# Second-product weights of a Mamba-style block in six buffers of two chunks instead of two buffers of six

## The chip, the cores and the metric

The kernel runs as one program on one core of a Trainium2 chip. The metric is the time of one execution on the device in microseconds (us); a change is judged by the median of repeated runs.

## What is computed

The input x is 8 images of 384 channels by 1024 positions, in fp32. One layer of two parts is applied:

```python
x = x + conv(ln_c(x), ...)          # the Mamba-style part, all 8 images
t = to_tokens(x)
t = t + ffn(ln_t(t), W1, b1, W2, b2)
x = from_tokens(t, x)
```

The first part normalises over channels twice, multiplies by in_proj (384 to 2 x 768), runs a causal convolution with 3 taps and SiLU over one half, derives step sizes and the rows B and C, and scans 16 states per inner channel along the 1024 positions:

```python
hst = dA_t * hst + dBu_t            # per position, 16 states per inner channel
y_t = einsum("bdn,bn->bd", hst, C_t)
y = (y + xc * D) * silu(z)
t = y @ out_proj_w.T                                        # 768 -> 384
t = gelu(t @ mlp_w1.T + mlp_b1) @ mlp_w2.T + mlp_b2         # 384 -> 1536 -> 384
```

The second part (FFN) binarises two weight matrices by the sign against a group mean, multiplies 384 to 1536, scales and clips by the largest absolute value, takes GELU, multiplies 1536 to 384 and scales and clips again. Only the first 5 of the 8 images get non-zero work in it.

## The kernel before, in words

**Tiling.** A matmul takes a 128x128 block of weights and 128x512 moving values in fp32. Channels lie on partitions in chunks of 128 (KC = 3 chunks of 384, KD = 6 of 768, KH = 12 of 1536, HK = 6 is half of KH), positions in two halves of T = 512. PER = 2 is the number of chunks in one activation tile: `split` (L459) makes a list of tiles of two chunks.

**Stages.** For each image b, `s1` (L670) normalises, multiplies by in_proj and makes xc, z, dt and dt*xc, and stores them to DRAM. `s2` (L835) with `scan` (L848) and `scan_pair` (L957) loads them back, spread over states, and scans on VectorE, with products on GpSimd (POOL), exponentials on ScalarE (ACT) and the sum over states on TensorE (tile `py`). `s3` (L1024) does out_proj (tile `p_out`), the first MLP product (`p_h`), GELU and the second MLP product (`p_o`). `ffn` (L1228) does the same for the FFN (`p_y`, which is written from `tn` in the first product and from `gf` in the second). `norm` (L590) is the normalisation used by `s1` and `ffn`.

**The order.** Nothing is issued in the order of the code. Each stage calls `Plan.add` (L201) with an engine, a cost in us, the tiles read and written and a function that emits the instructions. `Plan.run` (L248) is a list scheduler that runs while the program is built: it keeps a simulated time for PE, ACT, DVE, POOL and SP, takes the operation that can start first, picks among those able by `choose` (L274) and `rank` (L291: scans first, then the earliest batch), and emits it. The order in which it emits is each engine's program order on the chip; on the chip, semaphores hold every instruction until its inputs are there. A DMA in the plan costs its issue on SP, then `size / rate` on one shared transfer resource, then `land` (L370 to L373). Where the plan sees PE idle for over IDLE = 0.7 us, it fills the hole with small matmuls into a free PSUM tile named `spare` (L347 to L356, emitted at L451); their results are not used.

**Buffers.** `Ring` (L130) is a set of equal buffers. A tile takes one when its first operation starts and gives it back when the last operation that reads it has ended. Weights come through `weights` (L530), which makes one tile and one DMA load (`load`, L508, the load itself is L511, on SP). The rings of the two second products and of out_proj are made at L419; each buffer of six chunks holds 6 x 128 fp32 values per partition (384 KB in all), and the two rings hold two such buffers each:

```python
"w6": ring("w6", 2), "w6_n": ring("w6_n", 2), "res": ring("res", 4),
```

`w6` serves out_proj and the second MLP product, `w6_n` the FFN's second product and one third of out_proj in the last batch. In the profile their tiles are called `w` and `w_n`. The other products use tiles of three chunks, `w_f` and `w_b`.

**Where the tiles are used.** `mlp_out` (L1098) makes one PSUM tile from twelve chunks: it loads two tiles of six chunks, and adds three PE operations of two matmuls each per tile (`matmuls`, L536). So a weight tile is held until its third operation ends. out_proj adds one PE operation of six matmuls per output chunk (L1058 on); in the last batch five of the six matmuls are issued early, and the sixth when the scan's last tile is there (L1032 to L1054, the list `late`). The loads wait for a buffer, so SP, which issues in program order, stands at such a load until PE has read the old tile for the last time.

Of the kernel before, what the change touches and what calls it, by code (L numbers as in the profile page):

```python
# [35 lines left out]
KC = C // P  # L36
DI = 768
KD = DI // P
# [4 lines left out]
HK = KH // 2  # L43
PER = 2
T = 512
# [26 lines left out]
MM = 0.859  # L72
# [23 lines left out]
def c_dve(n):  # L96
    return 0.17 + n * 0.00102
# [71 lines left out]
class Fixed:  # L169


    ring = None
# [218 lines left out]
class Layer:  # L391
    def __init__(self, ctx, tc, a, out):
        self.tc, self.nc, self.a, self.out = tc, tc.nc, a, out
        self.plan = Plan()

        def pool(name, **kw):
            return ctx.enter_context(tc.tile_pool(name=name, bufs=1, **kw))

        self.const = pool("const")
        sbuf, psum, dram = pool("sbuf"), pool("psum", space=PSUM), pool("dram", space=DRAM)  # L400

        def ring(tag, bufs, where=sbuf):
            def make(shape, name):
                return where.tile(shape, F32, tag=tag, name=name, bufs=bufs)

            return Ring(make, bufs)

        self.rings = {

            "front": ring("front", 6), "t_f": ring("t_f", 2), "w_f": ring("w_f", 4),  # L410
            "dbc": ring("dbc", 1), "halo": ring("halo", 2),

            "dt_r": ring("dt_r", 2), "dtx_r": ring("dtx_r", 2), "u": ring("u", 3),
            "xr": ring("xr", 1), "zr": ring("zr", 1), "state": ring("state", 1),
            **{f"bc{i}": ring(f"bc{i}", 1) for i in range(2 * NQUAD)},
            "da": ring("da", 2, psum), "y": ring("y", 1, psum),

            "hid": ring("hid", 9), "t_b": ring("t_b", 1), "w_b": ring("w_b", 3),
            "w6": ring("w6", 2), "w6_n": ring("w6_n", 2), "res": ring("res", 4),  # L419

            "t_n": ring("t_n", 2), "small": ring("small", 4),

            "mm": ring("mm", 3, psum), "sq": ring("sq", 2),
            "rstd": ring("rstd", 2), "root": ring("root", 2),
        }

        def handed(name, shape):
            return Fixed(dram.tile(shape, F32, name=name))

        self.dram = {}  # L430
        for b in range(B):
            self.dram["dt", b] = handed(f"dt_d{b}", [DI, L])
            self.dram["dtx", b] = handed(f"dtx_d{b}", [KC, P, 2 * L])

            for name in ("xc", "z", "yg"):
                self.dram[name, b] = handed(f"{name}_d{b}", [KD, 2, P, T])
            self.dram["rows", b] = handed(f"rows_d{b}", [2 * NS, L])
            if b < NQ:
                self.dram["mid", b] = handed(f"mid_d{b}", [C, L])
                self.dram["y1", b] = handed(f"y1_d{b}", [P, KH, L])  # L440
        self.bin = {
            "W1": handed("bin_w1", [KH, P, KC, P]), "W2": handed("bin_w2", [KC, P, KH, P]),
        }
        self.constants()

        first = psum.tile([P, T], F32, tag="y", name="first", bufs=1)
        self.nc.tensor.matmul(
            first, self.ones, self.one.to_broadcast([P, T]), start=True, stop=True
        )
        self.plan.spare = self.piece("mm", [P, T], "spare")  # L450
        self.plan.fill = lambda: self.nc.tensor.matmul(  # L451
            self.plan.spare.real[:, : 2 * P], self.ones,
            self.one.to_broadcast([P, 2 * P]), start=True, stop=True,
        )
# [135 lines left out]
    def norm(self, t, eps, scale):  # L590

        nc, add = self.nc, self.plan.add
        def columns(src, name):
            p = self.piece("mm", [P, TG], name)

            def emit():
                for k in range(KC):
                    for g in range(G):
                        nc.tensor.matmul(
                            p.real[g * DQ : (g + 1) * DQ, :], self.ones[:, :DQ],  # L600
                            src.real[:, k, g * TG : (g + 1) * TG],
                            start=(k == 0), stop=(k == KC - 1),
                        )

            add("PE", 0.79, emit, r=[src], w=[p], tiled=True)
            return p

        def spread(src, name, turned=False):
            p = self.piece("mm", [P, T], name)

            def emit():
                for g in range(G):
                    if turned:
                        by, of = src.real[:, g : g + 1], self.ident
                    else:
                        by, of = self.ident[:, g * DQ : g * DQ + 1], src.real
                    nc.tensor.matmul(
                        p.real[:, g * TG : (g + 1) * TG], by.to_broadcast([P, P]), of,
                        start=True, stop=True,
                    )  # L620

            add("PE", 0.89, emit, r=[src], w=[p])
            return p

        total = self.piece("sq", [P, T], "total")
# [5 lines left out]
        def at_once():  # L631
# [1 line left out]
                total.real, t.real.rearrange("p k l -> p l k"), AX.X, ALU.add  # L633
            )

        add("POOL", 2.5, in_two, r=[t], w=[total], others={
            "DVE": (c_dve(KC * T) + 0.02, at_once)
        })
        p_mean = self.piece("mm", [P, T], "p_mean")
        add("PE", MM, lambda: nc.tensor.matmul(  # L640
            p_mean.real, self.ones, total.real, start=True, stop=True
        ), r=[total], w=[p_mean])
        add("DVE", c_dve(KC * T) + 0.05, lambda: nc.vector.scalar_tensor_tensor(
# [15 lines left out]
            r=[p_turned], w=[rstd])  # L659
# [364 lines left out]
    def s3(self, b):  # L1024
        nc, a, add = self.nc, self.a, self.plan.add
        yg_d = self.dram["yg", b]
        for half, cols in enumerate(HALVES):
            t2 = self.piece("t_b", [P, KC, T], "t2")
            if b == B - 1:
                yg = self.last_yg[half]  # L1030

                late = []  # L1032
                for m in range(KC):
                    w = self.weights("w6_n" if m == KC - 1 else "w6", KD, a["out_proj_last"][m],
                                     r=[yg[KC]])
                    pm = self.piece("mm", [P, T], "p_out")
                    self.matmuls(pm, w, yg, 0, KD - 1, True, False,
                                 [yg[k] for k in range(KD - 1)], [t2])
                    late.append((w, pm))
            else:  # L1040
                yg = self.split("hid", KD, "yg")
                for p, piece in enumerate(yg.pieces):
                    src = yg_d.real[p * PER : (p + 1) * PER, half].rearrange("k p l -> p k l")
                    self.plan.add(
                        "SP", 0.46, lambda piece=piece, src=src: nc.sync.dma_start(piece.real, src),
                        r=[yg_d[part] for part in yg_d.parts if part is not None
                           and part[:2] == (half, p)],
                        w=[piece[k] for k in range(PER)], claim=yg.pieces[p:],
                        size=4 * P * PER * T, land=2.0,
                    )  # L1050
            for m in range(KC):
                if b == B - 1:
                    w, pm = late[m]
                    self.matmuls(pm, w, yg, KD - 1, 1, False, True, [yg[KD - 1]], [t2], KD - 1)  # L1054
                else:
                    w = self.weights("w6", KD, a["out_proj_w"][m])
                    pm = self.piece("mm", [P, T], "p_out")
                    self.matmuls(pm, w, yg, 0, KD, True, True, [yg[k] for k in range(KD)], [t2])  # L1058
                self.affine(
                    lambda m=m, t2=t2: t2.real[:, m, :], lambda pm=pm: pm.real, [pm], [t2[m]]  # L1060
                )
            g = self.split("hid", KH, "g")
# [9 lines left out]
            for m in range(KC):  # L1072
# [1 line left out]
                res = self.piece("res", [P, T], "res")  # L1074

                self.load(res, lambda t: t, a["x"][b, rows, cols], r=[g[HK]], size=4 * P * T, land=2.3)
                po = self.mlp_out(lambda i, m=m: a["mlp_w2"][m, i], "w6", g, [res], "p_o")
                add("DVE", c_dve(T), lambda m=m, res=res, po=po: (
                    nc.vector.scalar_tensor_tensor(
                        res.real, po.real, self.mlp_b2[:, m : m + 1], res.real, ALU.add, ALU.add  # L1080
# [17 lines left out]
    def mlp_out(self, src, ring, g, claim, name, r=()):  # L1098

        po = self.piece("mm", [P, T], name)  # L1100
        for i in range(2):
            w = self.weights(ring, HK, src(i), r=r)
            for k in range(0, HK, PER):
                need = [g[i * HK + k + j] for j in range(PER)]
                self.matmuls(po, w, g, i * HK + k, PER, i + k == 0, i * HK + k + PER == KH, need,
                             claim, k)
        return po


# [118 lines left out]
    def ffn(self, b):  # L1228
# [32 lines left out]
        for h, cols in enumerate(HALVES):  # L1261
# [11 lines left out]
            y2.append(yh)  # L1273
            for m in range(KC):
                pm = self.mlp_out(
                    lambda i, m=m: w_d.real[m][:, i * HK : (i + 1) * HK, :], "w6_n", g, [yh], "p_y2",
                    r=[w_d[p] for p in need if p[1] == m],
                )
                self.affine(
# [125 lines left out]
```

## Time and profile before

| | us |
|---|---|
| median of 3 runs (lowest, highest) | 3203.15 (3200.61, 3204.09) |
| the profiled execution's own time | 3206.13 |
| its span | 3204.3 |
| PE busy | 3087.3 |
| POOL busy | 2803.7 |
| DVE busy | 2602.2 |
| ACT busy | 2021.0 |
| PE weight loads (PEld) busy | 1265.2 |

The span runs from the program's first instruction to the end of the last. An fp32 matmul appears as two records on PE, so the 576 matmuls of `p_o` are 1152 records. The records of a full 128x512 matmul start about 0.43 us apart when nothing holds them up (72 of them took 31.06 us in the last stretch), while each is shown as about 0.6 us long since they overlap. 2253 DMAs are issued on SP in the execution, and 751.78 MB are moved. The granted clock of TensorE is 0.987 over the execution.

### The profile page before, as it was taken

Reading aid. Unit: us, or ns where it says so; the run is one execution under the profiler, and the core shown is the slowest. Engines: PE = TensorE matmul, PEld = TensorE weight load, DVE = VectorE, ACT = ScalarE, POOL = GpSimd, SP = SyncE. Lnnn points to the kernel's source line nnn. Section 1 sums busy time; section 2 is a strip of 40 time slices with the busy share of each in tenths; the row PEclk is TensorE's granted clock in tenths of the full one; section 3 lists DMA queues with packets and bytes.
Section 4 is the critical chain, followed back from the end, with each engine's and each line's share of the span. In section 5 each row is a group of like instructions: output and inputs, shape, how many; then the busy total and the mean of one; then the engine's idle time right before and its main releaser. Section 6 shows DMA issues by size and latency. Waiting matters only on the chain.

```text
span 3204.3 us, 32487 instructions
## 1 busy us (share of the span) xinstructions
PE 3087.3 (96%) x10286; PEld 1265.2 (39%) x10286; DVE 2602.2 (81%) x2058; ACT 2021.0 (63%) x2397; POOL 2803.7 (87%) x1097
## 2 busy tenths in 40 slices
PE   9898999998999999999999999999999999999999
PEld 4333433343433443444344334343344443333333
DVE  4787887889978789787898888997788977887881
ACT  4878786767666565665675576457566565655662
POOL 2878988989989888999988999999989999998890
PEclk9899999999999999999999999999999999999999
DMA  7888878767777667766687686777768756756542
GB/s 236 293 290 303 272 230 305 267 213 250 241 287 249 202 204 248 261 229 221 207 296 239 212 301 213 253 229 278 239 223 268 235 184 216 232 179 191 162 153 72
DMA packets 348970, 751.78 MB, mean 235 GB/s; under 512 B 36480, under 2 KB 113792, under 8 KB 339584
## 3 DMA queue, kind: packets, MB, share of 16 engines
q1 hardware_dynamic: 348368, 749.61, 70.3%
q8 instruction: 83, 1.36, 0.2%
q14 instruction: 87, 0.71, 0.1%
q10 hardware_dynamic: 432, 0.09, 0.0%
HBM read 569.21 MB, written 180.36 MB: 234 GB/s over the span
## 4 chain that ended last, share of the span: by engine, by line
PE 62%; DVE 12%; DMA 9%; POOL 7%; ACT 6%; issue 3%; SPq 1%; DVEq 0%; POOLq 0%; ACTq 0%
PE p_y L541 15%; PE p_h L541 11%; PE p_o L541 10%; PE py L929 8%; PE p_out L541 6%; POOL u L965 5%; PE p_z L541 5%; PE p_in L541 5%; DVE u L990 4%; DVE da L990 3%; ACT da L557 2%; DMA dtx_r<-dtx_d 2%; ACT L557 2%; DMA dt_r<-dt_d 1%; PE spare L451 1%
## 5 line engine op out<-in xcount | busy, mean ns | idle before, releaser
L557 ACT ACTIVATE da<-dt_r,a_neg 128x1024 f32<-128x1024 f32 (+1 forms) x960 | 898.9, 944 | 596.0 <-DVE u L990 320.4
L965 POOL TENSOR_TENSOR u<-dtx_r,bc 128x2048 f32<-128x2048 f32 (+1 forms) x360 | 1185.5, 3309 | 87.6 <-PE py L929 49.1
L965 POOL TENSOR_TENSOR u<-u,bc 128x2048 f32<-128x2048 f32 (+1 forms) x274 | 900.0, 3291 | 140.9 <-DVE u L990 129.2
L990 DVE TENSOR_TENSOR_SCAN u<-da,u 128x1024 f32<-128x1024 f32 (+1 forms) x436 | 869.9, 2007 | 160.2 <-ACT da L557 80.6
L541 PE MATMUL p_h<-t,w_b 128*128 128x512 f32 x1152 | 515.7, 601 | 16.5 <-DMA w_b<-in_mlp_w 13.8
L541 PE MATMUL p_o<-g,w 128*128 128x512 f32 x1152 | 514.5, 600 | 6.4 <-DMA w<-in_mlp_w 4.7
L990 DVE TENSOR_TENSOR_SCAN da<-da,dtx_r 128x1024 f32<-128x1024 f32 (+1 forms) x192 | 382.0, 2015 | 64.0 <-POOL dtx_r L965 45.0
L965 POOL TENSOR_TENSOR dtx_r<-dtx_r,bc 128x2048 f32<-128x2048 f32 (+1 forms) x120 | 396.6, 3310 | 1.9
L541 PEld LDWEIGHTS p_h<-t,w_b 128*128 128x128 f32 x1152 | 215.0, 191 | 307.7 <-issue 264.0
L541 PEld LDWEIGHTS p_o<-g,w 128*128 128x128 f32 x1152 | 216.3, 191 | 298.0 <-issue 280.2
L541 PE MATMUL p_y<-tn,w_b 128*128 128x512 f32 x720 | 320.1, 600 | 7.7 <-DVE tn L664 3.4
L541 PE MATMUL p_y<-gf,w_n 128*128 128x512 f32 x720 | 321.9, 600 | 5.4 <-ACT dt L572 2.6
L929 PE MATMUL py<-u,fold 128*32 128x512 f32 x2304 | 306.7, 630 | 7.5 <-POOL u L965 7.5
L990 DVE TENSOR_TENSOR_SCAN da<-da,u 128x1024 f32<-128x1024 f32 (+1 forms) x140 | 281.8, 2038 | 34.0 <-ACT da L557 18.4
L557 ACT ACT_TABLE_LOAD x211 | 270.7, 1283 | 6.5 <-DMA dt_r<-dt_d 2.8
L541 PE MATMUL p_out<-yg,w 128*128 128x512 f32 x552 | 244.9, 596 | 3.4 <-ACT dt L572 1.8
L541 PE MATMUL p_in<-t,w_f 128*128 128x512 f32 x504 | 230.2, 605 | 15.5 <-ACT t L572 4.4
L541 PE MATMUL p_z<-t,w_f 128*128 128x512 f32 x504 | 232.4, 609 | 12.3 <-DMA w_f<-in_in_proj_w 7.7
L541 PEld LDWEIGHTS p_y<-tn,w_b 128*128 128x128 f32 x720 | 135.0, 191 | 189.5 <-issue 168.3
L541 PEld LDWEIGHTS p_y<-gf,w_n 128*128 128x128 f32 x720 | 134.6, 191 | 189.3 <-issue 170.9
L572 ACT ACTIVATE y<-p_y,v_vecs 128x512 f32<-128x512 f32 x145 | 98.8, 681 | 130.7 <-PE p_y L541 104.0
L572 ACT ACTIVATE g<-p_h,v_vecs 128x512 f32<-128x512 f32 x159 | 108.0, 679 | 114.1 <-PE p_h L541 113.6
(132 smaller groups left out, 3267.4 us busy)
## 6 DMA issues: line engine op xcount, KB each, us to landing
dtx_r<-dtx_d SPq DMA_DIRECT2D x72, 1024.0 KB, 6.0
dt_r<-dt_d SPq DMA_DIRECT2D x144, 512.0 KB, 5.1
w_b<-in_mlp_w SPq DMA_DIRECT2D x192, 192.0 KB, 3.4
w<-in_mlp_w SPq DMA_DIRECT2D x96, 384.0 KB, 3.3
w_f<-in_in_proj_w SPq DMA_DIRECT2D x168, 192.0 KB, 4.6
y_d<-y SPq DMA_DIRECT2D x120, 256.0 KB, 4.8
gf<-y_d SPq DMA_DIRECT2D x60, 512.0 KB, 6.7
xc_d<-xc SPq DMA_DIRECT2D x48, 512.0 KB, 6.5
```

What stands on the lines that cost most here:

```text
L451: self.plan.fill = lambda: self.nc.tensor.matmul(self.plan.spare.real[:, : 2 * P], self.ones, self.one.to_broadcast([P, 2 * P]), start=Tru ...
L541: self.nc.tensor.matmul(p.real, w.real[:, w0 + k, :], t.at(k0 + k), start=start and k == 0, stop=stop and k == n - 1,)
L557: lambda: self.nc.scalar.activation(out(), in_(), func, **{k: v() if callable(v) else v for k, v in kw.items()}),
L572: nc.scalar.activation(out(), in_(), AF.Identity, bias=bias, scale=scale)
L929: nc.tensor.matmul(py.real[g * DQ : (g + 1) * DQ, :], self.fold, hc, start=False, stop=(q == NQUAD - 1), skip_group_check=True,)
L965: nc.gpsimd.tensor_mul(u.real[:, x], t.real[:, x], row.real.unsqueeze(2).to_broadcast([P, n, 2]))
L990: da=da, in_u=in_u: nc.vector.tensor_tensor_scan(to(i), da.real[:, i, :], in_u(i), state.real[:, col : col + 1] if half else 0.0, ALU.mult ...
```

## The change

The two rings of two six-chunk buffers become two rings of six two-chunk buffers. They take the same space. `mlp_out` loads each pair of chunks by itself, as one tile with one DMA of 128 KB, and reads it in one PE operation. out_proj loads three tiles per output chunk; its one PE operation still makes all six matmuls and now reads three weight tiles. In the last batch only the last of the three tiles is kept for the late matmul. Five costs that the plan assumes for operations of `norm` are changed too; they change no instruction, only the plan's simulated times. Nothing in the diff or in either kernel is a table of ties: equal choices are still settled by `rank`.

```diff
-            "w6": ring("w6", 2), "w6_n": ring("w6_n", 2), "res": ring("res", 4),
+            "w2": ring("w2", 6), "w2_n": ring("w2_n", 6), "res": ring("res", 4),
...
-            add("PE", 0.79, emit, r=[src], w=[p], tiled=True)
+            add("PE", 0.68, emit, r=[src], w=[p], tiled=True)
...
-            add("PE", 0.89, emit, r=[src], w=[p])
+            add("PE", 0.98, emit, r=[src], w=[p])
...
-        add("POOL", 2.5, in_two, r=[t], w=[total], others={
-            "DVE": (c_dve(KC * T) + 0.02, at_once)
+        add("POOL", 2.64, in_two, r=[t], w=[total], others={
+            "DVE": (1.91, at_once)
         })
...
-        add("PE", MM, lambda: nc.tensor.matmul(
+        add("PE", MM + 0.08, lambda: nc.tensor.matmul(
...
                 for m in range(KC):
-                    w = self.weights("w6_n" if m == KC - 1 else "w6", KD, a["out_proj_last"][m],
-                                     r=[yg[KC]])
+                    ring = "w2_n" if m == KC - 1 else "w2"
                     pm = self.piece("mm", [P, T], "p_out")
-                    self.matmuls(pm, w, yg, 0, KD - 1, True, False,
-                                 [yg[k] for k in range(KD - 1)], [t2])
+                    for k in range(0, KD, PER):
+                        w = self.weights(ring, PER, a["out_proj_last"][m][:, k : k + PER, :],
+                                         r=[yg[KC]])
+                        n = min(PER, KD - 1 - k)
+                        self.matmuls(pm, w, yg, k, n, k == 0, False,
+                                     [yg[k + j] for j in range(n)], [t2])
                     late.append((w, pm))
...
-                    self.matmuls(pm, w, yg, KD - 1, 1, False, True, [yg[KD - 1]], [t2], KD - 1)
+                    self.matmuls(pm, w, yg, KD - 1, 1, False, True, [yg[KD - 1]], [t2], PER - 1)
                 else:
-                    w = self.weights("w6", KD, a["out_proj_w"][m])
                     pm = self.piece("mm", [P, T], "p_out")
-                    self.matmuls(pm, w, yg, 0, KD, True, True, [yg[k] for k in range(KD)], [t2])
+                    ws = [self.weights("w2", PER, a["out_proj_w"][m][:, k : k + PER, :])
+                          for k in range(0, KD, PER)]
+
+                    def whole(pm=pm, ws=ws, yg=yg):
+                        for k in range(KD):
+                            nc.tensor.matmul(pm.real, ws[k // PER].real[:, k % PER, :], yg.at(k),
+                                             start=k == 0, stop=k == KD - 1)
+
+                    add("PE", KD * MM, whole, r=[*ws, *(yg[k] for k in range(KD))], w=[pm],
+                        claim=[t2])
...
         for i in range(2):
-            w = self.weights(ring, HK, src(i), r=r)
             for k in range(0, HK, PER):
+                w = self.weights(ring, PER, src(i)[:, k : k + PER, :], r=r)
                 need = [g[i * HK + k + j] for j in range(PER)]
                 self.matmuls(po, w, g, i * HK + k, PER, i + k == 0, i * HK + k + PER == KH, need,
-                             claim, k)
+                             claim)
```

The callers in `s3` and `ffn` pass `"w2"` and `"w2_n"` where they passed `"w6"` and `"w6_n"`.

More of the change, by code (lines that the diff above doesn't have):

```diff
@@ L1076, in s3 @@
                 self.load(res, lambda t: t, a["x"][b, rows, cols], r=[g[HK]], size=4 * P * T, land=2.3)
-                po = self.mlp_out(lambda i, m=m: a["mlp_w2"][m, i], "w6", g, [res], "p_o")
+                po = self.mlp_out(lambda i, m=m: a["mlp_w2"][m, i], "w2", g, [res], "p_o")
                 add("DVE", c_dve(T), lambda m=m, res=res, po=po: (
@@ L1275, in ffn @@
                 pm = self.mlp_out(
-                    lambda i, m=m: w_d.real[m][:, i * HK : (i + 1) * HK, :], "w6_n", g, [yh], "p_y2",
+                    lambda i, m=m: w_d.real[m][:, i * HK : (i + 1) * HK, :], "w2_n", g, [yh], "p_y2",
                     r=[w_d[p] for p in need if p[1] == m],
```

## The prediction

> **What bounds the kernel now.** I read the page's first parts, then the chain and the groups, and then the tiles that the change touches. On the page:
>
> ```profile
> span 3204.3 us, 32487 instructions
> PE 3087.3 (96%) x10286; PEld 1265.2 (39%) x10286; DVE 2602.2 (81%) x2058; ACT 2021.0 (63%) x2397; POOL 2803.7 (87%) x1097
> PE   9898999998999999999999999999999999999999
> ...
> PE 62%; DVE 12%; DMA 9%; POOL 7%; ACT 6%; issue 3%; SPq 1%; DVEq 0%; POOLq 0%; ACTq 0%
> ...
> L541 PE MATMUL p_o<-g,w 128*128 128x512 f32 x1152 | 514.5, 600 | 6.4 <-DMA w<-in_mlp_w 4.7
> ```
>
> PE is busy in every slice and is 62% of the chain: TensorE bounds the kernel from end to end, and the change takes no matmul away. What can be won is time in which PE does nothing useful. That is 3204.3 - 3087.3 = 117 us of idle time and the filling matmuls of the plan, which the groups kept apart by shape give as follows (322 records, 81.3 us):
>
> ```profile
> L451 PE MATMUL spare<-small 128*128 128x256 f32 x322 | 81.3, 394 | 1.2 <-ACT z L570 0.9 <-DVE rstd L658 0.3
> ```
>
> So about 198 us, 6% of the span, is the whole reserve, from all causes. The share that belongs to these weights is in the views of tiles `w` and `w_n`, in the lists of what PE and its weight loader sat idle for (us, times):
>
> ```profile
>   DMA w<-in_mlp_w: 12.2, 14
>   DMA w<-in_out_proj_w: 3.5, 5
> ```
>
> ```profile
>   DMA w_n<-bin_w: 2.9, 6
> ```
>
> Together 18.6 us in 25 waits. How such a wait arises is seen near the end, in SP's timeline:
>
> ```profile
> 3078.01 1.17 SPq L858 DMA_DIRECT2D dtx_r<-dtx_d  x2
> 3079.97 1.73 SPq L886 DMA_DIRECT2D zr<-z_d  x4
> 3081.80 3.35 SPq L886 DMA_DIRECT2D xr<-xc_d  x4
> 3085.19 0.42 SPq L511 DMA_DIRECT2D w_n<-in_out_proj_last  x1
> 3085.71 0.38 SPq L511 DMA_DIRECT2D w_b<-in_mlp_w  x1
> 3086.19 8.05 SPq L511 DMA_DIRECT2D w<-in_mlp_w  x2
> ```
>
> and in PE's:
>
> ```profile
> 3080.52 8.75 PE L541 MATMUL p_o<-g,w 128*128 128x512 f32 x20
> 3090.21 8.82 PE L541 MATMUL p_o<-g,w 128*128 128x512 f32 x20 [0.94 <-DMA w<-in_mlp_w]
> ```
>
> PE has read its first tile at about 3080.5 + 12 x 0.43 = 3085.7; SP asks for the next contents at 3086.2; they land 3.9 us later (the chain has 3.89 us for this DMA), at 3090.1. Meanwhile PE has only the other tile to read; after 20 records it needs the new contents and stands idle for 0.94 us. The last line of SP's view is merged: its second load stands until the next tile is free.
>
> **What the Trainium skill says.** (1) "DMA: Bandwidth & Descriptors", section "Anatomy of one DMA", gives a DMA about 2.0 us of fixed cost and bytes/436e3 us for the data; an estimate from it is 2.9 us for 384 KB and 2.3 us for 128 KB. The page here shows 3.3 us for `w` (384 KB) and 3.4 us for `w_b` (192 KB): the fixed part rules, and is larger in this kernel's traffic. I price a load of 128 KB at 3.3 us, with the estimate of 2.3 us as the low end. (2) The same page, "Issuing engines are not separate DMA queues", calls the issuing time usually small against the DMA; the median issue of `w` is 0.333 us in the tile's view, a tenth of its landing, which agrees. (3) The same page, "Why a DMA increments its semaphore by 16 and not by 1", asks for one semaphore per DMA in flight. In this trace SP's 2253 issues carry eight semaphores in turn, so the ninth DMA waits for the first. SP's waits show it, for loads that read nothing of `dtx_r` (us in total, times, longest):
>
> ```profile
> SPq L511 <- PE p_o L541: 222.9, 74, 11.1
> SPq L886 <- DMA dtx_r<-dtx_d: 39.5, 32, 2.5
> SPq L511 <- DMA dtx_r<-dtx_d: 12.0, 7, 3.4
> ```
>
> (4) "Perfetto Trace Analysis", "Identifying the Most-Contended Engine", warns that PE's busy share overstates and asks for the weight loader's. It is 39%; a load of 0.19 us per record of 0.43 us would be 44% at full flow, so PE really runs at some 0.39/0.44 = 89%. That agrees with the 6% found above plus slower switches between shapes, which the change leaves alone.
>
> **The change part by part.**
>
> (a) *Deeper prefetch in `p_o` and in the FFN's second product.* Before, after a release, one tile is left: 6 x 0.86 = 5.2 us of work against 0.2 to 0.5 us until SP asks, plus 3.3 us, so 1.4 us of slack. After, a tile is released every two matmuls and five others are left: 10 x 0.86 = 8.6 us, a slack of about 4.8 us. A delay as at 3086 (lateness 0.9 us) fits in. Of the 18.6 us, some is not PE's: the loader runs one record ahead, so I take off 0.43 us for each of the 16 waits that were the loader's (9, 3 and 4 in the same views' lists of who waited), 6.9 us. 11.7 us are left, the upper end. out_proj's share of that, 3.5 - 3 x 0.43 = 2.2 us, stays, because its one operation holds three tiles to its end: its ring is again two sets. I take -9 us; ends -12 and 0 (if PE meets another wait at once, such as the GELU's output).
>
> (b) *What the plan can choose.* Its simulated ring comes free in thirds, and a product can start when 128 KB are there rather than 384 KB, a transfer of 0.4 us in place of 1.1 us by the plan's own rates. It will find a `p_o` or `p_y` for some holes it now fills with `spare`. Holes beside these products are seen in PE's timeline at 2601.8 (6.26 us), 2609.6 (3.65) and 3002.2 (about 2.8), though the first two end with GELU's output, so the weights alone don't open them. I take -6 us, 3% of the reserve of 198 us, as a choice; ends -15 and 0.
>
> (c) *Three DMAs for one.* The page and the list of DMAs have 96 + 42 + 4 loads of `w` and 60 + 2 of `w_n`: 204 become 612, so 408 more issues. 408 x 0.333 = 136 us of SP. SP is idle for most of the time: in the 40 us of a `p_o` stretch (1463.8 to 1503.8) its issues take about 8 us, and 12 more would add 4 us. On the path SPq is 1% of the span, 32 us, for some 900 us of issuing; at that share 136 us cost 4.8 us. Added waits for the eight semaphores: the two lines above are 51.5 us and the many others small; with 18% more DMAs some 20 to 30 us more on SP, at the same share 1 us. I take +5 us; ends 0 and +20, the upper if an eighth of those 165 us reaches PE. Queued behind each new wait on SP are the loads of `dt_r`, `dtx_r`, `xr` and `zr` of the scan; whoever waits for those is ACT and POOL, and PE only through `py`. Data volume does not change. Each DMA's 128 rows shrink from 3072 to 1024 bytes; at 70% busy DMA engines and 10% of the bytes I cost this at nothing, because PE's cover of 8.6 us hides it; without that cover it is tenths of a microsecond per load.
>
> (d) *New waits on PE.* Each two-matmul operation now waits for its own load besides its two activation chunks. It waited for the latter before, and 72 records of `p_o` in three-operation tiles ran in 31.06 us (0.431 each), so a satisfied wait costs nothing. The three waits ahead of out_proj's operation come once per six matmuls: nothing taken, +1 us at most.
>
> (e) *Five costs of the plan's `norm`.* No instruction changes. They move planned times by up to 0.15 us in 26 normalisations: zero, within 3 us either way.
>
> (f) *The order itself.* All planned starts move, so the program order does. The larger planned holes are single events (10.7 us of `spare` at 1310.0, 9.3 at 2551.9, 6.3 at 2601.8), and each can vanish or be joined by another. Taking them as independent, the root of the sum of squares of these and some twenty of 2 to 5 us is about 20 us. Its mean I take as zero, and it is most of my range.
>
> Sum: -9 - 6 + 5 = -10 us against the profiled execution's 3206.1 (span 3204.3 and 1.8 around it), so 3196. The median of the runs is 3.0 us under that execution: 3193 us, -0.3%.
>
> **The rivals.**
>
> *No difference (within 0.2%).* What ended a wait for weights was late because SP was behind; then PE next waits for `w_b` (its waits in `p_h` are 13.8 us, untouched) or GELU. (a) and (b) shrink to -5, (c) takes it back: 3203 us. For it: only 25 waits in 3204 us. Against it: the slack triples where PE works longest.
>
> *Slower: SP's eight semaphores.* In stretches with four-way loads (first and last image, as at 3080 to 3086) SP already stands for a landing of `dtx_r`, 6.0 us. With three loads per tile eight issues pass sooner, and a load of `w_b` or `dt_r` is asked for late. It decides from the point at which SP issues eight DMAs in under 6 us, which is 0.75 us each; the mean now is 3204/2253 = 1.42 us and becomes 1.20. Price: 165 us of SP at one eighth, +20, less 7 from (a): 3216 us. For it: SP stands at such loads already. Against it: the mean is well above 0.75 us.
>
> *A better order.* The re-planned order loses one of the holes of about 10 us and (b) reaches its end: -12 - 15 + 3 = -24 us: 3179 us. For it: 198 us of reserve; against it: nothing in the change addresses the holes at 1310 and 2552.
>
> **How the numbers follow.** Forecast (3185 to 3197) 0.38, better order 0.22, no difference 0.22, slower 0.18. A measurement of this kernel can tell about 0.2%, 6.4 us, from no change. Faster by more: 0.38 + 0.22 = 0.60; within: 0.22; slower: 0.18. The range for 8 in 10 runs from 3168 (better order with one more hole gone) to 3216 (the slower case's price).
>
> **What would show it.** Right: 612 loads of 128 KB, packets up from 348970 to about 407700 (204 x 256 more rows and 408 x 16 more semaphore writes) at the same 751.8 MB; waits for `w` and `w_n` down from 18.6 us to under 7; `spare` at or under 322 records; SPq's share of the chain still 1 to 2%. Wrong: waits of SP for landings above 100 us more, PE's waits for `w_b` well over 13.8 us, or idle time and `spare` together above 198 us although the waits for `w` fell; the last would mean that the order, not the weights, set the time.

## The result and the profile after

The changed kernel takes 3207.0 us in the median of nine runs (3199.1 to 3213.7), the kernel before 3203.15 us in nine runs beside them. The ratio is 1.001 with a 95% interval of 0.9996 to 1.0024: no difference that can be told. The profiled execution of the changed kernel took 3210.8 us, 4.7 us more than that of the kernel before. The time lies inside the range, 14 us over the forecast of 3193: it did not fall, and the rival "no difference" (3203 us) was nearest.

The page of the changed kernel, with the lines that answer to those of before:

```profile
span 3209.0 us, 33315 instructions
PE 3096.0 (96%) x10292; PEld 1266.8 (39%) x10292; DVE 2600.2 (81%) x2057; ACT 2026.7 (63%) x2407; POOL 2798.7 (87%) x1092
...
DMA packets 407729, 751.86 MB, mean 234 GB/s; under 512 B 43008, under 2 KB 198656, under 8 KB 398336
...
PE 60%; DVE 13%; POOL 9%; ACT 9%; DMA 5%; issue 4%; SPq 0%; DVEq 0%; POOLq 0%; ACTq 0%
...
L541 PE MATMUL p_o<-g,w 128*128 128x512 f32 x1152 | 510.1, 597 | 0.4 <-DMA w<-in_mlp_w 0.3
```

The packets are those foretold. PE's idle time ahead of `p_o` went from 6.4 to 0.4 us, of which loads of `w` had ended 4.7 us and now end 0.3: the second product hardly waits for weights any more. SP's own share of the chain did not grow. But the idle time of PE in all is 3209.0 - 3096.0 = 113 us against 117, and the filling matmuls are as many as before, as PE's groups kept apart by shape show:

```profile
L451 PE MATMUL spare<-small 128*128 128x256 f32 x328 | 81.5, 389 | 6.1 <-DVE xc L736 1.7 <-ACT dt L572 1.5 <-DVE t L643 1.1
```

In the view of tile `w`, the list of what PE and its weight loader sat idle for has three lines for its loads, and for `w_n` 0.5 us more:

```profile
  DMA w<-in_mlp_w: 9.0, 12
...
  DMA w<-in_out_proj_last: 3.0, 4
  DMA w<-in_out_proj_w: 2.0, 3
```

That is 14.5 us where 18.6 stood and under 7 was expected. But these lists add the idle time of two engines, and nearly all of it is the loader's, which can idle while PE works. PE's own waits for these weights, in the view of its waits (us in total, times, longest), were before:

```profile
PE p_o L541 <- DMA w<-in_mlp_w: 4.7, 5, 2.2
...
PE p_out L541 <- DMA w<-in_out_proj_w: 0.8, 2, 0.6
...
PE p_y L541 <- DMA w_n<-bin_w: 0.4, 2, 0.2
```

and after:

```profile
PE p_o L541 <- DMA w<-in_mlp_w: 0.3, 1, 0.3
...
PE p_out L541 <- DMA w<-in_out_proj_last: 0.3, 1, 0.3
```

So PE stood 5.9 us for these weights before and 0.6 us after. That is what deeper rings could take out of PE's idle time by themselves: 0.18% of the span.

**Where the time went.** Tables by stretches of 400 us tell it for the two profiled executions. Executions of the changed kernel differ by up to 15 us, so what follows accounts for the 4.7 us between these two, not for the medians. The columns are the stretch and its length, then the busy time of PE, PEld, DVE, ACT and POOL with instructions, PE's granted clock, the DMA share and GB/s. First the last two stretches of the kernel before:

```profile
2400.00:2800.00 400.00, 392.51 (x1307) 167.72 (x1299) 330.51 (x236) 237.87 (x256) 372.67 (x124) 1.00 0.70 228
2800.00:3204.00 404.00, 385.05 (x1153) 155.00 (x1152) 281.43 (x253) 212.42 (x306) 294.35 (x161) 0.99 0.49 152
```

and of the changed kernel:

```profile
2400.00:2800.00 400.00, 393.70 (x1330) 170.63 (x1328) 325.12 (x231) 236.48 (x257) 364.85 (x123) 1.00 0.68 224
2800.00:3209.00 409.00, 379.84 (x1113) 149.04 (x1112) 281.78 (x255) 207.32 (x300) 298.35 (x163) 0.97 0.49 148
```

Up to 2800 us, summed over the seven stretches, PE is idle 97.8 us before and 83.9 us after: it wins 13.9 us. Little of that comes from the weights: of PE's nine waits for them before, four lie ahead of 2800 us and make 0.8 us; the other five, 5.0 us, come later. The rest came with the new order, which the rings and the five costs wrote together. In the last stretch PE is idle 19.0 us before and 29.2 us after, and its clock is lower: 27 us of the stretch pass at half clock, against 10 us before. The two together more than take the 13.9 us back. PE's timeline at the very end shows for what it waits there. Before:

```profile
3127.53 4.56 PE L541 MATMUL p_out<-yg,w_n 128*128 128x512 f32 x10
3132.02 1.11 PE L929 MATMUL py<-u,fold 128*32 128x512 f32 x8
3132.94 1.85 PE L929 MATMUL py<-dtx_r,fold 128*32 128x512 f32 x8
3135.60 1.99 PE L541 MATMUL p_out<-yg,w 128*128 128x512 f32 x4 [0.80 <-DVE yg L942]
```

After:

```profile
3111.21 1.10 PE L929 MATMUL py<-dtx_r,fold 128*32 128x512 f32 x6 [1.39 <-DVE dtx_r L1012]
3117.60 3.78 PE L541 MATMUL p_out<-yg,w 128*128 128x512 f32 x4 [5.29 <-DVE yg L942]
...
3128.80 1.92 PE L929 MATMUL py<-u,fold 128*32 128x512 f32 x2 [4.15 <-POOL u L965]
...
3138.25 3.78 PE L541 MATMUL p_out<-yg,w 128*128 128x512 f32 x4 [0.80 <-DVE yg L942]
...
3143.32 31.06 PE L541 MATMUL p_h<-t,w_b 128*128 128x512 f32 x72
```

Before, PE has other matmuls until the last image's scan is done and waits 0.8 us for its last product `yg`. After, PE has run out of other work at 3110 and stands for 13.8 us in seven waits (four of them are in the lines above) for the products on POOL and DVE that finish the scan. The last `yg` ends at 3138.2 us, where it ended at 3135.5. From there only the last part of out_proj, 36 matmuls of `p_h` and 36 of `p_o` are left, which need each other: 68.8 us before. After it is 70.8: with PE's clock down after those waits, the four records at 3138.25 take 3.78 us where they took 1.99. So 4.7 = 2.7 (the scan ends later) + 2.0 (a slower start of the tail). What PE won earlier, it spent on waiting and on the half clock. Why the scan ended no earlier in the new order is not shown.

### The profile page after: what moved, and what is told of

The parts are those of the page before. It is cut to its first block, busy times and chain, and to the rows that moved or that the text cites. A ratio compares the mean times of both kernels' runs of the same rounds, so it can differ in the third digit from the quotient of the medians.

```text
span 3209.0 us, 33315 instructions
## 1 busy us (share of the span) xinstructions
PE 3096.0 (96%) x10292; PEld 1266.8 (39%) x10292; DVE 2600.2 (81%) x2057; ACT 2026.7 (63%) x2407; POOL 2798.7 (87%) x1092
## 4 chain that ended last, share of the span: by engine, by line
PE 60%; DVE 13%; POOL 9%; ACT 9%; DMA 5%; issue 4%; SPq 0%; DVEq 0%; POOLq 0%; ACTq 0%
PE p_y L541 13%; PE p_o L541 12%; PE p_h L541 11%; PE py L929 7%; POOL u L965 7%; PE p_z L541 5%; DVE u L990 5%; PE p_in L541 4%; DVE da L990 4%; PE p_out L1065 3%; ACT da L557 3%; ACT L557 2%; POOL dtx_r L965 1%; PE p_dt L801 1%; DVE xc L736 1%
## 5 line engine op out<-in xcount | busy, mean ns | idle before, releaser
L541 PE MATMUL p_h<-t,w_b 128*128 128x512 f32 x1152 | 515.2, 600 | 14.6 <-DMA w_b<-in_mlp_w 11.8
L1065 PE MATMUL p_out<-yg,w 128*128 128x512 f32 x504 | 224.4, 599 | 2.3 <-DVE t L577 2.3
L1010 DVE TENSOR_TENSOR dtx_r<-da,bc 128x1024 f32<-128x1024 f32 x144 | 171.8, 1216 | 0.5
```

The costliest lines, as they stand in the source:

```text
L541: self.nc.tensor.matmul(p.real, w.real[:, w0 + k, :], t.at(k0 + k), start=start and k == 0, stop=stop and k == n - 1,)
L1010: nc.vector.tensor_mul(u.real[:, 0, :, t], da.real[:, 0, :], cq.real)
L1065: nc.tensor.matmul(pm.real, ws[k // PER].real[:, k % PER, :], yg.at(k), start=k == 0, stop=k == KD - 1)
```

## The experiments

Theory A: the deeper prefetch does take away the waits for weights, but the order that the planner writes anew decides the time. Theory B: the 408 added DMAs on SP eat the gain. Theory C: waits for weights were never worth anything. All times are against the kernel before in the same session. The last three columns are of the one profiled execution of each kernel, whose time can lie several us off the median (before 3206.1, e1 3196.2, e2 3207.0, e8 3199.7): when the last `yg` ended, how long the execution went on after that, and what PE itself stood for `w` and `w_n` (the lines of its waits, added up).

| kernel | median, us | ratio (95%) | mean clock | last yg, us | after it, us | PE for w, w_n, us |
|---|---|---|---|---|---|---|
| before | 3202.9 to 3204.5 | | 0.987 | 3135.5 | 68.8 | 5.9 |
| changed | 3207.0 | 1.001 (0.9996 to 1.0024) | 0.987 | 3138.2 | 70.8 | 0.6 |
| e1 same order, three DMAs | 3200.0 | 0.9994 (0.9986 to 1.0001) | 0.987 | 3125.6 | 68.8 | 1.7 |
| e2 costs only | 3199.9 | 0.9994 (0.9986 to 1.0002) | 0.990 | 3136.2 | 68.8 | 7.5 |
| e3 rings only | 3211.1 | 1.0025 (1.0014 to 1.0035) | 0.983 | 3110.3 | 96.2 | 0.0 |
| e4 four buffers | 3201.1 | 0.9995 (0.9985 to 1.0005) | 0.988 | 3132.2 | 68.8 | 9.4 |
| e5 four in turn | 3203.6 | 1.0002 (0.9992 to 1.0011) | 0.988 | 3134.3 | 68.8 | 7.3 |
| e6 changed, in turn | 3208.5 | 1.0012 (0.9999 to 1.0024) | 0.987 | 3137.9 | 68.8 | 3.5 |
| e7 before, nudged | 3235.7 | 1.0101 (1.0083 to 1.0118) | 0.982 | 3138.4 | 96.3 | 6.3 |
| e8 changed, nudged | 3205.1 | 1.0005 (0.9994 to 1.0015) | 0.988 | 3101.7 | 96.2 | 0.0 |
| e9 e2 with three DMAs | 3198.2 | 0.998 (0.9972 to 0.9988) | 0.990 | 3128.1 | 68.8 | 6.2 |
| e10 e7 with three DMAs | 3237.4 | 1.0106 (1.0089 to 1.0123) | 0.982 | 3139.9 | 96.2 | 1.2 |
| e11 before, nudged again | 3191.9 | 0.9958 (0.9944 to 0.9972) | 0.988 | 3117.5 | 69.2 | 8.4 |
| e12 changed, nudged again | 3207.4 | 1.0009 (1.0001 to 1.0017) | 0.988 | 3108.7 | 96.3 | 1.7 |

PE's waits for the weights do not go with the time: the fastest kernel, e11, has more of them than the kernel before, and the slowest, e10, hardly any.

**e1: the DMAs alone.**

```diff
+                return Thirds([sbuf.tile([P, PER, P], F32, tag=tag, name=name, bufs=6)
+                               for _ in range(KD // PER)])
...
-            "w6": ring("w6", 2), "w6_n": ring("w6_n", 2), "res": ring("res", 4),
+            "w6": thirds("w6"), "w6_n": thirds("w6_n"), "res": ring("res", 4),
...
+                for i, t in enumerate(w.real.tiles):
+                    self.nc.sync.dma_start(t, src[:, i * PER : (i + 1) * PER, :])
```

> The kernel before with its order on every engine kept, operation for operation, but each weight tile of six chunks made of three tiles of two, loaded by three DMAs one after the other at the place of the one. 408 DMAs more, no other change. Theory A (the new order gives back what the weights won): -3 to +3 us against before. Theory B (the added DMAs and their semaphores on SP eat the gain): +8 to +12 us. Theory C (waits for weights cost nothing, PE meets the next wait at once): -2 to +2 us.

Measured -0.06%, interval from -0.14% to +0.01% (the medians differ by 2.9 us). Theory B, +8 to +12 us, falls: whatever 408 DMAs more cost in an unchanged order, it is hardly more than what they gain. More is to be seen. Here no tile is loaded earlier or held shorter in the plan, and still the idle time before `p_o` fell, from 6.4 to 3.4 us, and that for its loads from 4.7 to 1.7:

```profile
L567 PE MATMUL p_o<-g,w 128*128 128x512 f32 x1152 | 510.3, 596 | 3.4 <-DMA w<-in_mlp_w 1.7 <-ACT dt L598 1.6
```

```profile
  DMA w<-in_mlp_w: 5.9, 10
```

PE's own waits for these weights are 1.7 us in place of 5.9, most of what the changed kernel reached, at the old order. A first third of 128 KB lets PE begin sooner. But on the chip the thirds are also six buffers that come free one by one, and SP's waits for `p_o` fell from 222.9 to 142.6 us; so e1 does not part the smaller piece from an earlier release.

**e2: the five costs alone.**

```diff
-            add("PE", 0.79, emit, r=[src], w=[p], tiled=True)
+            add("PE", 0.68, emit, r=[src], w=[p], tiled=True)
...
```

> The kernel before with only the five planned costs of the normalisation changed; no tile and no DMA changes, the order does. Theory A: anywhere in -15 to +15 us against before, with other holes in PE's timeline and waits for w still about 18 us in the views of the tiles. Theories B and C: -3 to +3 us, since nothing is loaded otherwise.

Measured -0.06%, not clear of zero. The waits for `w` and `w_n` in the two lists stayed (23.0 us). It does not tell the theories apart by time. Its filling matmuls went from 322 to 404 records, so the order is another one.

**e3: the rings alone.**

```diff
-            add("PE", 0.68, emit, r=[src], w=[p], tiled=True)
+            add("PE", 0.79, emit, r=[src], w=[p], tiled=True)
...
```

> The changed kernel with the five planned costs put back; the two-chunk rings stay. Theory A: anywhere in -15 to +15 us against before, away from the changed kernel's +3.9 by several us, while PE's waits for w stay under 3 us. Theories B and C: within 3 us of the changed kernel, so 0 to +7 us against before.

Measured +0.25%, clear of zero and 4 us over the changed kernel. This speaks for A, weakly. The table shows something else: its last `yg` ends 25 us earlier than before, and 96.2 us follow it in place of 68.8. The scan was early, but PE still had 32 matmuls (27.4 us) of `p_o` and out_proj to do that it owed. PE's own waits for the weights are gone (0.0 us), and the kernel is slower all the same.

**e4 and e5: more buffers at the old order.**

```diff
-            "w6": ring("w6", 2), "w6_n": ring("w6_n", 2), "res": ring("res", 4),
+            "w6": shared(), "w6_n": shared(), "res": ring("res", 4),
```

`shared` gives both rings the same four buffers, while the plan counts 2 + 2.

> The kernel before with its order on every engine kept, operation for operation, but the two rings of two six-chunk buffers share one set of four buffers on the chip, while the plan still counts two and two. No DMA more; where only one of the two products runs, its loads no longer wait for PE's last release. Theories A and B: the waits for w fall from 18.6 us to under 8, and the time falls by 4 to 9 us. Theory C: the waits for w fall as much, the time stays within 2 us.

In e5 each load takes from these four the one that has been free longest.

> As e4 (order of the kernel before kept on every engine, four six-chunk buffers in common), but a load takes the buffer that has been free longest, not the one just freed, so it hardly ever waits for PE. No DMA more. If the first step of the prediction holds (loads come late because they wait for PE's last release): waits for w under 8 us in the views of the tiles and 3 to 9 us less time than before. If loads come late because SP reaches them late: waits for w stay at 14 to 22 us, time within 2 us of before and of e4.

Neither moved the time, nor the waits: 21.6 us in the two lists in e4, 18.6 us in e5 (13.1 + 2.4 + 3.1). All theories had expected under 8 us for e4; e5 came out as was expected if SP reaches the loads late. It is not a clean test, since SP's waits for `p_o` fell only from 222.9 to 131.4 and 134.5 us; probably each ring's own next tiles fill the shared buffers as soon as they are free, so that a spare one is rare. What these runs do show is that the long stalls stay at the same four places in the last images. In e4 the loads for which PE waited there (1.41 us at 2823, 1.10 at 2910, 2.20 at 3001, 2.46 at 3085) were issued at once after SP's issue ahead of them, without any wait for a buffer: SP came to them late, behind bursts of `xr`, `zr`, `dt_r` and `w_b`. In the trace of before the five stalls whose load SP issued without a wait make 5.0 of the 5.9 us that PE stood for these loads. SP asked there 2.0, 1.0, 1.8, 4.6 and 0.4 us after PE had read the old tile for the last time; in all but the last, the one at 3090 us, that is more than the stall itself. A deeper ring at the same place in SP's order can't help those.

**e6: the changed kernel with buffers taken in turn.**

```diff
-            "w2": ring("w2", 6), "w2_n": ring("w2_n", 6), "res": ring("res", 4),
+            "w2": turns(), "w2_n": turns(), "res": ring("res", 4),
```

`turns` gives both rings the same twelve buffers and takes the one that has been free longest.

> The changed kernel with its order on every engine kept, its two rings of six two-chunk buffers sharing twelve, the longest free taken first. If SP standing at PE's releases held up the other loads in the changed kernel (theory B): 4 to 8 us less than the changed kernel, so -4 to 0 us against before. If its loss lies in the order (theory A): within 2 us of the changed kernel, +2 to +6 us against before.

SP's waits for `p_o` fell from 217.0 to 129.6 us, the time did not follow (+0.12%, the changed kernel +0.1%). So SP's standing at PE's releases is not what holds the changed kernel.

**e7, e8, e11, e12: other orders out of the same planner.** One planned cost is moved by 0.01 us, which changes no instruction:

```diff
-        add("PE", 0.14, lambda: nc.tensor.matmul(
+        add("PE", 0.15, lambda: nc.tensor.matmul(
...
```

(e7; in e8 and e11 the `tensor_scalar_add` on DVE has 0.16 for 0.15, in e12 the power on POOL 1.01 for 1.00.)

> The kernel before with one planned cost nudged (p_turned 0.15 for 0.14 us): another order out of the same planner, the same tiles and loads. Theory A: anywhere in -10 to +10 us against before, as a sample of what a re-planning alone does. Theories B and C: within 2 us.

> The changed kernel with one planned cost nudged (the addition ahead of the power 0.16 for 0.15 us): another order with the two-chunk rings. Theory A: anywhere in -10 to +10 us against before, not tied to the changed kernel's +4. Theories B and C: within 2 us of the changed kernel, +2 to +6 us against before.

> The kernel before with another planned cost nudged (the addition ahead of the power 0.16 for 0.15 us): one more order with the six-chunk tiles. Theory A: 0 to +30 us against before, the spread that e7 showed. If e7 was a single accident: within 5 us of before.

> The changed kernel with the planned cost of the power nudged (1.01 for 1.00 us): one more order with the two-chunk rings. If these rings make any order good: within 5 us of the changed kernel's +4, like e3 and e8. If their orders spread as those of the six-chunk tiles: anywhere in -5 to +30 us against before.

The two orders with six-chunk tiles went to +1.01% and -0.42%. Those with the two-chunk rings (changed, e3, e8, e12) lie between +0.05% and +0.25%. A hundredth of a microsecond in a planned cost thus moves the kernel by -13 to +32 us, where all of PE's waits for these weights are 5.9 us. Theories B and C expected 2 us for e7, and A at most 10, so all were too narrow. e11 missed its expectation on the good side. It is faster than both kernels, with the old tiles, and PE stands longer for `w` and `w_n` than before (8.4 us against 5.9). What it has is a last scan that ends 18 us earlier in its profiled execution, with no matmuls left over: 69.2 us follow.

In e7 the scan ends 3 us later than before, and PE's debt comes on top. PE is idle for 132 us against 117 and busy for 15 us longer. Half clock holds for 113 us against 82, which is 15 us of PE's time by itself. The new holes are not the weights'; the largest is in the normalisation, here in e7 and then before:

```profile
PE p_var L599 <- ACT sq L557: 17.2, 7, 5.2
```

```profile
PE p_var L599 <- ACT sq L557: 5.8, 4, 2.9
```

e8 shows the other kind of end, in PE's timeline:

```profile
3100.82 15.72 PE L541 MATMUL p_o<-g,w 128*128 128x512 f32 x36
3116.38 8.75 PE L541 MATMUL p_out<-yg,w 128*128 128x512 f32 x20
3124.96 4.46 PE L541 MATMUL p_out<-yg,w_n 128*128 128x512 f32 x10
...
3132.26 31.06 PE L541 MATMUL p_h<-t,w_b 128*128 128x512 f32 x72
```

Its last `yg` ended at 3101.7, 34 us before that of the kernel before. PE took it up only at 3129, after 36 records of `p_o` and 30 of out_proj that were still owed. The early scan alone is worth nothing either.

**e9 and e10: three DMAs at two more orders.** The edit of e1 on e2 and on e7.

> The order of e2 (kernel before with the five planned costs) kept on every engine, with each six-chunk tile made of three tiles loaded by three DMAs in the same place, as in e1. If three small loads are worth something at any order, as e1's -3 us hints: 2 to 6 us under e2, so -4 to -9 us against before. If they are worth nothing: within 2 us of e2, -4 to 0 us against before. Under theory B: 8 us over e2.

> The order of e7 (kernel before, p_turned nudged, +32 us) kept on every engine, with the three tiles and three DMAs of e1. If three small loads are worth something at any order: +26 to +30 us against before. If nothing: +30 to +34 us. In no case does it come near before, since the loss is in the order.

e9 came out at 0.998 where e2 had 0.9994, as expected if small loads are worth something; e10 at 1.0106 where e7 had 1.0101, as expected if they are worth nothing. With e1 the three pairs give about -2, -4 and +2 us, taken from ratios whose intervals are 2 to 6 us wide on either side. So no cost of three small loads shows at any order, and a gain of a few us is possible but not shown. In e10 PE's waits for `w` and `w_n` are down to 1.2 us (6.3 us in e7), and the time is not: its end is the one with 96.2 us, PE's debt.

Theory A is left, with one point of C: the waits for weights are some 6 to 9 us of PE's time, too little to be told from the scatter of the orders.

## Why the prediction was right or wrong, step by step

That the time lies in the range is the range's doing: it is 48 us wide because of (f), and the change that was forecast, -10 us, did not come.

*What bounds the kernel.* This is where it failed. "TensorE bounds the kernel from end to end" was read off a full row of nines and 62% of the chain; and so (a) and (b) were taken off the total at full value. In truth two ends have to be met: the last scan and what follows it (68.8 us), and PE's sum of work. In the kernel before they meet within 0.8 us, as its trace shows. By the traces a gain on PE alone turns into a wait for the scan, as in the changed kernel; a gain in the scan alone turns into a debt of PE, as in e3, e8 and e12. The rival "no difference" foresaw that PE would meet its next wait, but named `w_b` (13.8 us before, 11.8 after) and GELU, not the last scan. Its other half, that loads were late because SP was behind, is what the trace of before shows. This account of the two ends is read from the traces: no run shortened the scan or PE's sum alone, and that POOL or DVE holds the scan was not tried.

*(a) Deeper prefetch, -9 us.* Near in size, but not by its working. The 18.6 us are PE's idle time, 5.9 us in nine waits, plus its loader's, 12.7 us in sixteen; seven of the nine fall at the same moment as one of the loader's, so one wait was counted twice. Taking 0.43 us off each of the loader's left 11.7 us as the upper end, where PE's own lines have 5.9 us. Those went to 0.6 us. What the waits cost in all can be estimated: records of 0.6 us that start 0.43 us apart hide about 0.17 us of each, which makes 7.4 us of nine, and one of them, at 3005 us, was followed by 3.4 us at half clock, another 1.7. So about 9 us were there to be won if every one of them went; that the figure taken was the same is luck. The slack was wrong too: "0.2 to 0.5 us until SP asks" holds at 3086, but it was 1.0 to 4.6 us at the other four of the five later stalls. What removed them, depth, the place of the loads in SP's new order or the smaller piece, is not told apart: e1 had most of it (5.9 to 1.7 us) without a new order. The 13.9 us that PE wins up to 2800 us are mostly not from here.

*(b) What the plan can choose, -6 us.* `spare` stands at 81.5 us against 81.3, in 328 records where at most 322 were expected: nothing. With PE's idle time it is 194.5 us, just under the 198 that were named as a sign of the order.

*(c) Three DMAs for one, +5 us.* e1, e9 and e10 show no cost, each together with whatever the smaller pieces gain. The landings that hold up SP through the eight semaphores grew little, by the same two lines as before:

```profile
SPq L886 <- DMA dtx_r<-dtx_d: 44.5, 36, 2.1
...
SPq L511 <- DMA dtx_r<-dtx_d: 16.2, 11, 2.8
```

These two are 9.2 us more, but all of SP's waits for landings together went from 281 to 248 us, where 20 to 30 us more were expected, and no more of SP is on the chain. The rival "slower" is out. The price of a 128 KB load, 3.3 us, was near: the page has 3.0 us for `w` from `mlp_w`. The low end of 2.3 us was too low: the fit that it is from, in "DMA: Bandwidth & Descriptors" of the Trainium skill, "Anatomy of one DMA", is for DMAs issued from GpSimd, and these go out on SP.

*(d) New waits on PE.* Right: the 72 records of `p_o` at the end take 31.06 us in both kernels.

*(e) The five costs, within 3 us.* Alone (e2) right: -0.06%. With the rings they change the order and go with a difference of some 4 us (e3 against the changed kernel).

*(f) The order.* Rightly given most of the range, and still too small on one side: a root of squares of 20 us stood against +32 us (e7) and -13 us (e11) from a nudge of 0.01 us. With four orders for each kind of tile, the means are about +4 us for both. Whether the two-chunk rings make orders less scattered, as it looks, is open.

## What to carry to other kernels

A row of full slices doesn't show that an engine's savings will reach the end: look at the last dependent stretch, what it waits for, and whether another chain arrives there at the same moment. Before pricing a wait, take the waits of the engine itself; its loader's idle time is not to be added. If what is left is about what a measurement can tell (here 5.9 us, against the 6.4 of the prediction), the time can hardly judge the change. Where a planner writes the order, a change of buffers is tested by holding the order and changing the loads (e1), and by nudging the planner without changing anything (e7, e11); without both, a fraction of a per cent tells nothing about the buffers. Splitting a load into parts with buffers of their own can take away most of such waits at an unchanged order (e1).

## What the runs showed of the hardware

408 more DMAs on one queue, 18% of all, cost no time that could be measured, net of what their smaller pieces gain (e1: -0.14% to +0.01%), although SP's DMAs share eight semaphores in turn.

The granted clock adds to what a hole costs. It stands at 0.50 in pieces of 3.4 us and multiples, 96 us in all in the changed kernel's trace and 106 us in e3's, against 82 us before. The length and the half agree with "TensorE: Matmul & The Clock Gate", Part 1 in the Trainium skill, which gives the gate a window of about 3.4 us and half the clock after an idle one. But shorter holes were enough here: in the changed kernel the clock falls at 3135.4 us after 3.4 us of which PE was busy for 1.6 (it stood in two waits of 0.58 and 1.37), and in the kernel before at 3006.1 us after a single wait of 2.15 us for `w`. e3's mean clock over its runs, 0.983 against 0.987, is at most 0.004 x 3211 = 13 us of PE's time, more than its whole loss of 8 us; that the clock caused the loss is inferred, not tried.
